# A conditioned transformer block on one Trainium2 core: another order of the products inside a block of tokens, and another place for the residual rows of odd blocks

## The chip, the cores and the metric

The kernel runs on one core of one Trainium2 chip. Its engines are TensorE (PE in the profile, its weight loads PEld), VectorE (DVE), ScalarE (ACT), GpSimd (POOL) and SyncE (SP), which issues nearly all the transfers here. The metric is the device time of one execution in microseconds (us). The time before is the median of three runs.

## What is computed

x has 8 sequences of T = 1024 tokens and D = 512 features, in float32. A condition vector for each sequence gives six modulation vectors. The reference, cut to its core:

```python
mod = silu(condition) @ Wada + bada
sh_a, sc_a, gt_a, sh_m, sc_m, gt_m = split(mod, 6, axis=1)
xm = layernorm(x, g1, be1) * (1 + sc_a) + sh_a
q, k, v = split(xm @ Wqkv)              # 16 heads of 32 features
a = softmax(causal(q @ k.T / sqrt(32))) @ v
x = x + gt_a * (a @ Wproj + bproj)
xm = layernorm(x, g2, be2) * (1 + sc_m) + sh_m
x = x + gt_m * (gelu(xm @ W1 + b1) @ W2 + b2)   # 512 -> 2048 -> 512, exact gelu
```

## The kernel before

**Tiles.** The work is cut into NB = 16 blocks of TB = 512 tokens, two for a sequence. An even block n is the first half of its sequence, an odd block the second half, whose queries also attend to the keys of the even block before it. Each linear product (q, k, v, the attention's projection, the four up products u0 to u3 of the MLP) is done with seven half-size products instead of eight, by sums of operands (Strassen-Winograd, `strassen`, L896; its last two products run as a side thread, `tail`). The sums of the weights are made once and kept in DRAM; "preps" and "sums" steps make them in the first windows. The four down parts d0 to d3 (`down`, L1196) take differences of the hidden tiles hT (L1211) and add their partial results to the residual rows. `matmul` (L205) issues four matmuls side by side on columns of TensorE; each is two records in the trace ("128*32" is this column form, "32*128" the row form of the attention's products over 32 features).

**Weights** come in pieces of 256 KB, in the order of the plan, on SP's queue into a ring of nine buffers "w" (`fetch`, L336 to L348). A buffer is loaded again when its piece is released.

**Attention** of a block goes through four groups of four heads (`attend`, L1824). For a group: scores in PSUM (L1602); DVE masks the diagonal units (L1616) and reduces each query's maximum (L1619; L1633 joins the two halves' maxima for odd blocks); the maxima are split into three bf16 parts (`split_maxima`, L1638 to L1641), on POOL or on DVE, whichever the planner's clocks say; TensorE turns them into rows (L1657) and ACT copies those (L1663). Then the transposed weights: the negative maxima are added by a product (L1683), the scores by another (L1695), ACT takes the exponential (L1708), POOL clears above the diagonal (L1713). TensorE multiplies by v (L1736), POOL or DVE add the weights up (L1821, L1818). Their sums come out of a product with ones (L1757) into one of three PSUM banks "l", which the linear products share; ACT takes the logarithm of it (L1767), copies the result (L1770), takes the exponential of the negative logarithm (L1775), and the product with that replaces the block's qT. For the last groups DVE does a part of that (L1782).

**Order of the work.** The kernel writes its instructions out in an order fixed while it is built. A hand-written `plan[w]` (L234) lists the linear steps of windows -1 to 16: in window w stands the attention of block w, and beside it go linear steps of the blocks around it. A planner keeps an estimated clock for each engine (`now`, `note`, `due`) and, before each attention step, lets linear work go ahead until the attention's next operand should be there or until the linear work done keeps pace with the planned share (`step_aside`, `pace`, `linear_wait`). `either` (L154) puts an addition of two tiles on DVE (L162) or POOL (L165) by the same clocks. GELU goes to ACT in excursions of four (L1153), each between two loads of a function table (L1153, L145).

Steps of a window: "load_xr" fetches the four residual tiles of a block (L1353); "proj" projects and adds the residual, which also gives the second norm's statistics (L628, L637 to L640, L653); "mt" transposes the normed rows (L769) and applies the modulation (L778, L784), with the sums for the fast products (L792, L794); "at" does that for the first norm of a later block; "load_xa" and "norm_a" fetch and norm its rows. In the plan of before, an odd window w takes the steps left over, v of w, load_xr and proj of w-1, k of w+1, mt, q of w+1, u0 to u3, at, d0, d1; an even one begins with the left d2, d3, and leaves its u3, at and d's to the next.

**Buffers.** Key tiles kT have three buffers of one pool in turn; residual rows have one buffer "xr", which only the rows of block 14 leave for a key buffer. A step waits by flags such as "free for k", which `attend` sets when the attention of a block begins.

Of the kernel before, what the change touches and what calls it, by code (L numbers as in the profile page):

```python
# [22 lines left out]
def kernel(  # L23
# [36 lines left out]
    P = 128  # L60
# [177 lines left out]
        0: [("load_xa", 2), ("preps",), ("k", 1), ("norm_a", 2), ("gates", "a"), ("q", 1)]  # L238
        + [("mod", 4), ("at", 2), ("v", 1), ("mod", 3), ("gates", "m")],
    }  # L240
    late = []
    for w in range(1, NB):
        n = w - 1
        m = mlp_steps(n)
        even = blocks[n][1] == 0
        rows_a = [("rows", blocks[n][0], "a")] if even else []
        rows_m = [("rows", blocks[n][0], "m")] if even else []
        own = m[:1] + ([("load_xa", w + 2)] if w + 2 < NB else []) + m[1:3]
        own += [("norm_a", w + 2)] if w + 2 < NB else []
        if w == NB - 1:  # L250
            steps = late[:1] + [("load_xr", n)] + rows_a + [("proj", n), ("mt", n)] + late[1:]
            steps += [("v", w)] + rows_m + own + m[3:6]
            late = m[6:]
        else:

            steps = late + [("v", w), ("load_xr", n)] + rows_a + [("proj", n), ("k", w + 1)]
            if w == 1:
                steps = [("load_xr", n)] + rows_a + [("k", w + 1), ("proj", n)]
            steps += [("mt", n), ("q", w + 1)] + rows_m + own
            at = [("at", w + 2)] if w + 2 < NB else []  # L260
            if blocks[w][1] == 0:

                late = m[3:4] + at + m[4:]
            else:
                steps += m[3:4] + at + m[4:6]
                late = m[6:]
        plan[w] = steps
    n = NB - 1
    plan[NB] = [("load_xr", n), late[0], ("beside", ("proj", n)), late[1], ("mt", n)] + mlp_steps(n)

    plain_proj = (NB - 2, NB - 1)
    kept_sums = {}
# [538 lines left out]
        return bank  # L811

    qTs, kTs, vs = {}, {}, {}
    projected, valued = set(), set()
    xm_of, hTs, hidden = {}, {}, set()

    SUMS = (("S1", "A21", "A22", ALU.add), ("S2", "S1", "A11", ALU.subtract),
# [78 lines left out]
    def strassen(step, x, dest, target, row, done, put=None, after={}):  # L896
# [91 lines left out]
        tail_key[0] = key  # L988
        start(tail())

    def project_T(step, store, pool, tag, done):

        n = step[1]
        dst = pool.tile([P, NC, TB], F32, tag=tag, name=f"{tag}_{n}")
        store[n] = dst
        yield from strassen(
            step,
            f"a{n}",
            lambda f, t: dst[:, half(f, 2), half(t, HB)],
            (tag, n),  # L1000
            False,
            done,
        )
# [326 lines left out]
    def perform(step):  # L1330
# [12 lines left out]
        elif kind == "load_xr":  # L1343
            n = step[1]
            b, h = blocks[n]
            if n == NB - 2:
                xr = kvp.tile([P, NTT, D], F32, tag="kT", name=f"xr_{n}")
            else:
                xr = xrp.tile([P, NTT, D], F32, tag="xr", name=f"xr_{n}")
            residual[n] = xr  # L1350
            for t in range(NTT):
                r0 = h * TB + t * P
                nc.sync.dma_start(xr[:, t, :], x[b, r0 : r0 + P, :])  # L1353
                landed = max(now["PE"], stored.get(n, 0.0)) + LANDING + 700 * t
                written["xr", n, t] = landed
        elif kind == "norm_a":
            key = f"a{step[1]}"
# [5 lines left out]
        elif kind == "beside":  # L1363
            start(perform(step[1]))
        elif kind == "sums":
            sum_weights(step[1:])
        elif kind == "mt":
            n = step[1]
            guards = [("v done", n + 1)]
            start(modulated(f"m{n}", *columns_of["m"], blocks[n][0], guards))  # L1370
        elif kind == "k":
            yield [("free for k", step[1])], []
            yield from project_T(step, kTs, kvp, "kT", lambda: None)
        elif kind == "q":
# [449 lines left out]
    def attend():  # L1824
        previous = None
        for n in range(NB):
# [19 lines left out]
            stream["rate"] = planned_time(n) / mine * (0.7 if n == 0 else 1.0)  # L1846
            written["free for k", n + 2 if n % 2 else n + 1] = 0.0
            written["free for k", n + 1] = 0.0
            for g, k, n_slots, upto in slots:
                if (n, g) == groups[-1]:  # L1850
                    margin[0] = -2000
# [47 lines left out]
            finish(n, g)  # L1899

    def next_scores():
        until(lambda: units[unit_at[0]][0] in projected)
        scores(*units[unit_at[0]])
        unit_at[0] += 1

# [12 lines left out]
    needs = sum(exp_need(parts) for n in range(NB) for g in range(NC) for parts in weight_units(n, g))  # L1918
    needs += sum(score_need(*unit) for unit in units)
    for n in range(NB):  # L1920
        written["attended", n] = NEVER
# [81 lines left out]
```

## Time and profile before

| | before |
|---|---|
| runs, median (range) | 3483.92 us (3483.72 to 3483.95) |
| profiled execution | 3487.44 us |
| its span | 3485.7 us |
| outside the span | 1.7 us |
| instructions on DVE, ACT, POOL | 2136, 1420, 2209 |
| bytes moved | 466.84 MB |

The profile is of one execution. Its page gives each engine's busy time and share of the span, 40 slices with the TensorE clock that was granted, the chain of work that ended last, and the costliest groups of instructions. The trace behind it answers further views: waits (engine, line waited for, total us, times, longest), windows (busy time of each engine in a stretch of time, then the granted clock, the share of DMA time and GB/s), and a timeline (start, duration, engine, line, operation, output and input; in brackets the idle time of the engine just before, and what ended it). Rows of a timeline on TensorE overlap a little, since matmuls are pipelined: the time that a group costs is the next row's start less its own.

### The profile page before, as it was taken

The page shows a single profiled execution, that of the slowest core. Times are in us where ns is not written, and L with a number is a line of the kernel's source. Part 1 is how long each engine was busy: PE and PEld are TensorE (multiplying, and loading weights), DVE is VectorE, ACT ScalarE, POOL GpSimd, SP SyncE. Part 2 cuts the span into 40 slices and gives each one's busy share as a digit, 9 for nine tenths or more (in the row PEclk, how much of TensorE's full clock was granted, in tenths as well). Part 3 has the DMA queues.
Part 4 walks back from the last instruction along what each step waited for, and adds up shares of the span by engine and source line. Part 5 has one row for each costly group of instructions (what it writes and reads, how often), then busy time and mean ns, then how long its engine had stood idle before and what let it go on. Part 6 is the DMA issues. An engine that isn't in the chain of part 4 may idle for free.

```text
span 3485.7 us, 122756 instructions
## 1 busy us (share of the span) xinstructions
PE 3448.3 (99%) x55618; PEld 1776.1 (51%) x55618; DVE 1905.0 (55%) x2136; ACT 1286.7 (37%) x1420; POOL 2074.5 (60%) x2209
## 2 busy tenths in 40 slices
PE   8999999999999999999999999999999999999999
PEld 5544455445554554545545455454554545545445
DVE  6765664554645556465564655645546455554463
ACT  2335243352433524235152352514524244241531
POOL 3676755675466664576645766557664576644640
PEclk9999999999999999999999999999999999999999
DMA  6843334335353353633536335363443534435334
GB/s 213 271 144 86 117 110 150 120 105 172 107 167 102 105 174 104 186 95 100 173 98 186 98 111 159 101 186 98 129 140 101 183 101 135 130 100 153 90 121 136
DMA packets 350523, 466.84 MB, mean 134 GB/s; under 512 B 27460, under 2 KB 212092, under 8 KB 350004
## 3 DMA queue, kind: packets, MB, share of 16 engines
q1 hardware_dynamic: 349808, 458.73, 43.8%
q8 instruction: 438, 7.18, 0.9%
q14 instruction: 81, 0.66, 0.1%
q10 hardware_dynamic: 196, 0.28, 0.0%
HBM read 416.90 MB, written 41.99 MB: 132 GB/s over the span
## 4 chain that ended last, share of the span: by engine, by line
PE 94%; DVE 3%; POOL 1%; ACT 1%; issue 0%; DMA 0%; SPq 0%; DVEq 0%; ACTq 0%; POOLq 0%
PE bank L205 65%; PE sc L1602 9%; PE po L1736 8%; PE st L1695 7%; PE st L1683 3%; DVE mx L1619 2%; PE bank L1757 2%; PE bank L769 1%; PE bank L1657 1%; POOL pT L1821 0%; DVE sc L1616 0%; POOL mcols L1640 0%; DVE pT L1818 0%; POOL mcols L1641 0%; DMA ada<-in_L_cond_Wada_dram 0%
## 5 line engine op out<-in xcount | busy, mean ns | idle before, releaser
L1821 POOL TENSOR_TENSOR pT<-pT,pT 128x256 f32<-128x256 f32 (+3 forms) x1254 | 1174.5, 972 | 210.3 <-ACT pT L1708 119.2
L1708 ACT ACTIVATE pT<-st 128x2048 f32<-128x2048 f32 x288 | 541.1, 1879 | 1001.1 <-PE st L1695 908.8
L205 PE MATMUL bank<-w,hT 128*32 128x256 f32 x14336 | 795.5, 379 | 0.0
L1619 DVE TENSOR_REDUCE mx<-sc 128x4 f32<-128x2048 f32 (+3 forms) x384 | 665.6, 1754 | 140.3 <-PE sc L1602 133.7
L205 PEld LDWEIGHTS bank<-w,hT 128*32 128x32 f32 x14336 | 448.8, 110 | 335.6 <-issue 29.2
L205 PE MATMUL bank<-xm_m,w 128*32 128x256 f32 x8192 | 498.8, 380 | 0.0
L205 PE MATMUL bank<-t_m,w 128*32 128x256 f32 x6144 | 384.2, 380 | 0.1
L205 PEld LDWEIGHTS bank<-xm_m,w 128*32 128x32 f32 x8192 | 253.6, 110 | 238.8 <-issue 76.0
L1713 POOL TENSOR_SCALAR_AFFINE_SELECT pT<-pT 128x512 f32<-128x512 f32 x256 | 164.8, 661 | 308.8 <-ACT pT L1708 306.9
L1602 PE MATMUL sc<-kT,qT 32*128 32x512 f32 (+3 forms) x3072 | 329.1, 520 | 2.9 <-DVE mx L1619 1.9
L1616 DVE TENSOR_TENSOR sc<-sc,mask 128x1024 f32<-128x1024 f32 (+1 forms) x160 | 162.9, 1018 | 276.2 <-PE sc L1602 217.6
L1736 PE MATMUL po<-pT,v 128*32 128x512 f32 (+3 forms) x3072 | 306.0, 493 | 0.0
L1695 PE MATMUL st<-qT,kT 32*128 32x512 f32 (+3 forms) x3072 | 299.8, 486 | 0.0
L205 PEld LDWEIGHTS bank<-t_m,w 128*32 128x32 f32 x6144 | 193.0, 110 | 180.8 <-issue 54.2
L205 PE MATMUL bank<-xm_a,w 128*32 128x256 f32 x3968 | 248.8, 381 | 1.3 <-ACT xm_a L784 1.1
L197 DVE TENSOR_TENSOR hT<-bank,u_u 128x512 f32<-128x512 f32 x192 | 129.1, 686 | 151.2 <-PE bank L205 149.0
L165 POOL TENSOR_TENSOR qT<-top,rec 128x512 f32<-128x512 f32 x60 | 77.1, 1285 | 219.8 <-ACT rec L1775 219.8
L1602 PEld LDWEIGHTS sc<-kT,qT 32*128 32x128 f32 x3072 | 129.4, 183 | 150.9 <-ACT pT L1708 61.8
L205 PE MATMUL bank<-w,qT 128*32 128x256 f32 (+1 forms) x2944 | 191.4, 399 | 1.3 <-DVE qT L1782 1.3
L1153 ACT ACTIVATE hT<-hT,cols 128x512 f32<-128x512 f32 x256 | 164.2, 711 | 55.0 <-DVE hT L197 54.4
L205 PE MATMUL bank<-t_a,w 128*32 128x256 f32 x2944 | 183.3, 380 | 0.0
L165 POOL TENSOR_TENSOR hT<-hT,hT 128x1024 f32<-128x1024 f32 x28 | 79.7, 2868 | 167.6 <-DVE hT L1211 167.6
(232 smaller groups left out, 3507.5 us busy)
## 6 DMA issues: line engine op xcount, KB each, us to landing
w<-in_L_cond_W_dram SPq DMA_DIRECT2D x384, 256.0 KB, 2.9
w<-kept_up_S SPq DMA_DIRECT2D x256, 256.0 KB, 2.6
w<-kept_down_S SPq DMA_DIRECT2D x256, 256.0 KB, 2.8
w<-kept_qkv_S SPq DMA_DIRECT2D x180, 256.0 KB, 2.7
w<-in_L_cond_Wqkv_dram SPq DMA_DIRECT2D x147, 256.0 KB, 3.0
hat<-in_x_dram SPq DMA_DIRECT2D x64, 256.0 KB, 4.7
xr<-in_x_dram SPq DMA_DIRECT2D x64, 256.0 KB, 4.6
out_dram<-xr SPq DMA_DIRECT2D x64, 256.0 KB, 2.6
```

Source lines behind the costliest of these rows:

```text
L165: nc.gpsimd.tensor_tensor(out, a, b, op)
L197: nc.vector.tensor_tensor(out, src, other, op)
L205: nc.tensor.matmul(ps[r, :], lhsT[:, r], rhs, start=start, stop=stop, skip_group_check=True)
L1153: nc.scalar.activation(hT[:, i, :], hT[:, i, :], AF.Gelu, bias=cols[:, O_B1 + f : O_B1 + f + 1])
L1602: nc.tensor.matmul(sc[:, j, c0 : c0 + w], qTs[n][r, gg, ts(qt, P)], keys_of(n, kh)[r, gg, :w], start=True, stop=True, skip_group_check=True,)
L1616: nc.vector.tensor_tensor(place, place, shape_of.to_broadcast(place.shape), ALU.add)
L1619: nc.vector.tensor_reduce(maxima[n, gg][:, kh, qt, :], sc[:, :, c0 : c0 + w], axis=AX.X, op=ALU.max)
L1695: nc.tensor.matmul(st[:, j, c0 : c0 + w], kT[r, gg, ts(k % NTT, P)], qT[r, gg, TB - w :], start=False, stop=True, skip_group_check=True,)
L1708: nc.scalar.activation(pT[:, :, :used], st[:, :, :used], AF.Exp, scale=scale)
L1713: nc.gpsimd.affine_select(diagonal, diagonal, pattern=[[0, HPG], [1, P]], compare_op=ALU.is_ge, fill=0.0, base=0, channel_multiplier=-1,)
L1736: nc.tensor.matmul(po[r, TB - w :], v[:, k % NTT, g * P + j * hd : g * P + (j + 1) * hd], pT[:, j, c0 : c0 + w], start=(k == 0), stop=last ...
L1821: nc.gpsimd.tensor_tensor(into, into, pT[:, j, c0 : c0 + w], ALU.add)
```

## The change

The plan of windows 1 to 15 is put in another order, so that the four down parts of a block stand together. In the new plan an odd window w (from 3) has: the left u2, u3 and "at"; load_xr and v; proj and mt of block w-1; d0 to d3 of block w-2; q, then k, of block w+1; u0 to u3 of w-1 with load_xa and norm_a among them; at. An even window has the same without the left steps ahead, and stops after u1 of its block, which leaves u2, u3 and at to the next window. In window 15, which has no q and k to make, d0 and d1 of block 14 come at the end; windows 1 and 2 lead over from the order of the first ones, and window 16 is as it was.

Key tiles get buffers by name: one for odd blocks and two for even blocks in turn. The residual rows of an odd block go into the even key buffer that is free at that time, for which load_xr waits for a new flag "free for xr"; the rows of even blocks use "xr". `next_scores` also asks that the keys are done, since k now comes after q. The planner's estimate of when residual rows land uses the stores of the block before.

```diff
+        at = [("at", w + 2)] if w + 2 < NB else []
+        ups = m[:1] + ([("load_xa", w + 2)] if w + 2 < NB else []) + m[1:3]
+        ups += ([("norm_a", w + 2)] if w + 2 < NB else []) + m[3:4] + at
+        head = rows_a + [("load_xr", n)]
+        if w == 1:
+            steps = head + [("k", w + 1), ("proj", n), ("mt", n), ("q", w + 1)]
+        elif w == 2:
+            steps = downs[2:] + [("v", w)] + head + [("proj", n), ("mt", n), ("q", w + 1), ("k", w + 1)]
+        elif w < NB - 1:
+            steps = late + head + [("v", w), ("proj", n), ("mt", n)] + downs + [("q", w + 1), ("k", w + 1)]
+        else:
+            steps = late + head + [("v", w), ("proj", n), ("mt", n)] + downs
+        cut = m[2] if blocks[w][1] == 0 else None
+        i = ups.index(cut) if cut in ups else len(ups)
+        plan[w] = steps + rows_m + ups[:i]
+        late, downs = ups[i:], m[4:]
+        if w == 1:
+            plan[w] += downs[:2]
         if w == NB - 1:
-            steps = late[:1] + [("load_xr", n)] + rows_a + [("proj", n), ("mt", n)] + late[1:]
-            steps += [("v", w)] + rows_m + own + m[3:6]
-            late = m[6:]
-        else:
-
-            steps = late + [("v", w), ("load_xr", n)] + rows_a + [("proj", n), ("k", w + 1)]
-            if w == 1:
-                steps = [("load_xr", n)] + rows_a + [("k", w + 1), ("proj", n)]
-            steps += [("mt", n), ("q", w + 1)] + rows_m + own
-            at = [("at", w + 2)] if w + 2 < NB else []
-            if blocks[w][1] == 0:
-
-                late = m[3:4] + at + m[4:]
-            else:
-                steps += m[3:4] + at + m[4:6]
-                late = m[6:]
-        plan[w] = steps
+            plan[w] += late + downs[:2]
+            downs = downs[2:]
     n = NB - 1
-    plan[NB] = [("load_xr", n), late[0], ("beside", ("proj", n)), late[1], ("mt", n)] + mlp_steps(n)
+    plan[NB] = [("load_xr", n), downs[0], ("beside", ("proj", n)), downs[1], ("mt", n)] + mlp_steps(n)
...
+    def key_tag(n):
+        return "odd_kT" if n % 2 else f"even_kT_{n // 2 % 2}"
...
-        dst = pool.tile([P, NC, TB], F32, tag=tag, name=f"{tag}_{n}")
+        if tag == "kT":
+            dst = pool.tile([P, NC, TB], F32, tag=key_tag(n), name=f"{tag}_{n}", bufs=1)
+        else:
+            dst = pool.tile([P, NC, TB], F32, tag=tag, name=f"{tag}_{n}")
...
-            if n == NB - 2:
-                xr = kvp.tile([P, NTT, D], F32, tag="kT", name=f"xr_{n}")
+            if n % 2:
+                yield [("free for xr", n)], []
+                spare = key_tag(min(n + 3, NB))
+                xr = kvp.tile([P, NTT, D], F32, tag=spare, name=f"xr_{n}", bufs=1)
             else:
                 xr = xrp.tile([P, NTT, D], F32, tag="xr", name=f"xr_{n}")
...
-                landed = max(now["PE"], stored.get(n, 0.0)) + LANDING + 700 * t
+                landed = max(now["PE"], stored.get(n - 1, 0.0)) + LANDING + 700 * t
...
-            yield from project_T(step, kTs, kvp, "kT", lambda: None)
+            yield from project_T(step, kTs, kvp, "kT", lambda: keyed.add(step[1]))
...
+            written["free for xr", n - 1] = 0.0
...
-        until(lambda: units[unit_at[0]][0] in projected)
+        until(lambda: units[unit_at[0]][0] in projected & keyed)
```

More of the change, by code (lines that the diff above doesn't have):

```diff
@@ L240 @@
     }
-    late = []
+    late, downs = [], []
     for w in range(1, NB):
@@ L247 @@
         rows_m = [("rows", blocks[n][0], "m")] if even else []
-        own = m[:1] + ([("load_xa", w + 2)] if w + 2 < NB else []) + m[1:3]
-        own += [("norm_a", w + 2)] if w + 2 < NB else []
-        if w == NB - 1:
-            steps = late[:1] + [("load_xr", n)] + rows_a + [("proj", n), ("mt", n)] + late[1:]
-            steps += [("v", w)] + rows_m + own + m[3:6]
-            late = m[6:]
-        else:
-            steps = late + [("v", w), ("load_xr", n)] + rows_a + [("proj", n), ("k", w + 1)]
-            if w == 1:
-                steps = [("load_xr", n)] + rows_a + [("k", w + 1), ("proj", n)]
-            steps += [("mt", n), ("q", w + 1)] + rows_m + own
-            at = [("at", w + 2)] if w + 2 < NB else []
-            if blocks[w][1] == 0:
-                late = m[3:4] + at + m[4:]
-            else:
-                steps += m[3:4] + at + m[4:6]
-                late = m[6:]
-        plan[w] = steps
+        at = [("at", w + 2)] if w + 2 < NB else []
[16 more added lines that the diff above has]
+            plan[w] += downs[:2]
+        if w == NB - 1:
+            plan[w] += late + downs[:2]
+            downs = downs[2:]
     n = NB - 1
-    plan[NB] = [("load_xr", n), late[0], ("beside", ("proj", n)), late[1], ("mt", n)] + mlp_steps(n)
+    plan[NB] = [("load_xr", n), downs[0], ("beside", ("proj", n)), downs[1], ("mt", n)] + mlp_steps(n)
     plain_proj = (NB - 2, NB - 1)
@@ L813 @@
     qTs, kTs, vs = {}, {}, {}
-    projected, valued = set(), set()
+    projected, keyed, valued = set(), set(), set()
     xm_of, hTs, hidden = {}, {}, set()
@@ L1920 @@
     for n in range(NB):
+        written["free for xr", n] = 0.0 if n == NB - 1 else NEVER
         written["attended", n] = NEVER
```

## The prediction

> **What bounds the kernel now.** I read the page first, for the engine that fills the span.
>
> ```profile
> span 3485.7 us, 122756 instructions
> PE 3448.3 (99%) x55618; PEld 1776.1 (51%) x55618; DVE 1905.0 (55%) x2136; ACT 1286.7 (37%) x1420; POOL 2074.5 (60%) x2209
> PEclk9999999999999999999999999999999999999999
> PE 94%; DVE 3%; POOL 1%; ACT 1%; issue 0%; DMA 0%; SPq 0%; DVEq 0%; ACTq 0%; POOLq 0%
> ```
>
> TensorE is busy for 99% of the span at the full granted clock (all nines), and 94% of the chain that ended last is its own work. A new order of the same products can only win back its idle time. The windows view says how much there is, stage by stage (columns: window, length, then PE's busy time):
>
> ```profile
> 920.00:1348.00 428.00, 426.64 (x6952) 219.37 (x6944) 229.95 (x258) 162.15 (x178) 263.47 (x279) 1.00 0.45 132
> 1348.00:1776.00 428.00, 426.64 (x6948) 219.37 (x6944) 230.04 (x259) 161.45 (x177) 263.00 (x279) 1.00 0.45 132
> 3150.00:3400.00 250.00, 246.69 (x3884) 126.19 (x3880) 126.79 (x138) 89.93 (x104) 130.59 (x123) 1.00 0.39 118
> ```
>
> A pair of blocks (even, then odd) takes 428 us, repeats exactly, and leaves 428.00 - 426.64 = 1.36 us of idle time; the tail window leaves 3.31 us. The waits view of one pair names it (total us, times, longest):
>
> ```profile
> PE bank L1657 <- POOL mcols L1641: 0.7, 1, 0.7
> PE bank L769 <- ACT xm_m L784: 0.3, 1, 0.3
> PE sc L1602 <- DVE mx L1619: 0.2, 1, 0.2
> ```
>
> The timeline shows why the longest of them, for the split maxima, is late, and prices a few things used below:
>
> ```profile
> 980.76 1.15 PE L1602 MATMUL sc<-kT,qT 32*128 32x384 f32 x16
> 981.84 1.50 PE L205 MATMUL bank<-t_m,w 128*32 128x256 f32 x24
> 982.05 1.23 DVE L1616 TENSOR_TENSOR sc<-sc,mask 128x1024 f32<-128x1024 f32 x1 [0.89 <-PE sc L1602]
> 983.16 2.77 PE L205 MATMUL bank<-w,hT 128*32 128x256 f32 x48
> 983.32 2.35 DVE L1619 TENSOR_REDUCE mx<-sc 128x4 f32<-128x1536 f32 x2
> 985.87 0.40 PE L1683 MATMUL st<-mrow,minus_ones 32*128 32x384 bf16 x8
> 986.40 2.35 DVE L1211 TENSOR_TENSOR hT<-hT 128x1024 f32<-128x1024 f32 x2
> 986.57 1.16 POOL L1640 CAST mcols<-rest 128x16 bf16<-128x16 f32 x1
> 988.93 0.41 PE L1657 MATMUL bank<-ident_b,mcols 128*32 128x128 bf16 x16 [0.74 <-POOL mcols L1641]
> 989.16 2.12 PE L205 MATMUL bank<-w,hT 128*32 128x256 f32 x36
> ```
>
> Scores end, DVE masks and reduces, POOL splits the maxima while DVE's two L1211 run, and TensorE has only 6.2 us of other work meanwhile. Two prices: a linear record costs (983.16 - 981.84) / 24 = 0.055 us; and since neighbouring rows overlap (988.93 + 0.41 ends 0.18 us after 989.16), a wait loses that overlap too. With it the pair's stalls cost about 0.92 (maxima), 0.38 (transposes L769), 0.25 and 0.18 (scores waiting for the reduction): 1.73 us.
>
> **What the change moves.** I count in the order of each engine's instructions as the changed kernel is built. TensorE's order is the same up to about 555 us of this trace, then differs in every block to the end, with the same matmuls in the same forms. Forms alternate a little more: 17 more column-to-row switches, each about 0.07 us (the 48 records from 983.16 to 985.87 take 2.71 where 48 x 0.055 is 2.64), at most 1.2 us, and 15 fewer runs of transposes, whose switches work the other way: between -1 and 1.2, and I take +0.1, since the two counts nearly cancel. The weights are the same; so are the DMAs, 1721.
>
> *What goes.* In an odd block 9.2 us of TensorE work, not 6.2, now lie between scores and the maxima's use, so the 0.92 goes; the second norm's transposes come with other work around them (0.38), and the scores of both blocks follow later (0.25 + 0.18). Six places each: 6 x 1.73 = 10.4 us. The tail's own stalls:
>
> ```profile
> 3203.66 1.89 PE L769 MATMUL bank<-ident,xh_m 128*128 128x128 f32 x13 [0.31 <-ACT xh_m L653]
> 3334.71 0.40 PE L1683 MATMUL st<-mrow,minus_ones 32*128 32x512 bf16 x4 [1.52 <-ACT pT L1708]
> 3358.86 1.07 PE L205 MATMUL bank<-w,qT 128*32 128x512 f32 x8 [1.07 <-DVE qT L1782]
> 3360.14 2.35 PE L205 MATMUL bank<-w,qT 128*32 128x512 f32 x20 [0.21 <-DVE qT L1782]
> ```
>
> With overlap and switches they cost about 0.8, 1.6 and 1.9, with 0.5 of smaller ones 4.8 us; they go because block 14's down products now stand behind the second norm and some 32 us of them between the last attention and its projection. Gain at most 10.4 + 4.8 = 15.2 us, 0.4% of the span. That is the bound below, since nothing but idle time can be won.
>
> *What is late instead.* Five pairs (blocks 5/6 to 13/14) repeat one order.
>
> A, odd block, third group: behind its last score unit stand 48 linear records (2.7 us) where the trace above has 24 + 48. The chain there, 981.84 to 985.87, takes 4.03 us: mask, two reductions, hops. Late 1.1 to 1.3; I take **1.2**.
>
> B, even block, second group: a bank is freed by the logarithm L1767, behind an exponential and a GELU excursion in ACT's queue:
>
> ```profile
> 1202.99 1.88 ACT L1708 ACTIVATE pT<-st 128x2048 f32<-128x2048 f32 x1 [1.62 <-PE st L1695]
> 1204.88 1.28 ACT L1153 ACT_TABLE_LOAD   x1
> 1206.18 2.56 ACT L1153 ACTIVATE hT<-hT,cols 128x512 f32<-128x512 f32 x4
> 1208.76 1.28 ACT L145 ACT_TABLE_LOAD   x1
> 1215.72 0.57 ACT L1767 ACTIVATE rec<-bank 128x512 f32<-128x512 f32 x1
> 3339.37 1.07 PE L1736 MATMUL po<-pT,v 128*32 128x512 f32 x8
> ```
>
> 1.88 + 1.28 + 2.56 + 1.28 + 0.57 = 7.6, with hops 7.7; TensorE has 72 linear records (3.9), a score unit (981.84 - 980.76 = 1.1), one weighted sum (1.07 less the 0.18 of overlap, 0.9) and the sums of L1757, of the same size (0.9): 6.8. Late **0.9**; the hops are not shown for this place, so 0.5 to 1.2.
>
> C, odd block, first to second group: one full reduction behind two combines and a small offset, against 64 records (3.6 us):
>
> ```profile
> L1619 DVE TENSOR_REDUCE mx<-sc 128x4 f32<-128x2048 f32 x192 | 439.6, 2290 | 137.0 <-PE sc L1602 133.7
> L197 DVE TENSOR_TENSOR hT<-bank,u_u 128x512 f32<-128x512 f32 x192 | 129.1, 686 | 151.2 <-PE bank L205 149.0
> ```
>
> 2.29 + 2 x 0.69 + hops = 3.7 to 4.1: late 0.1 to 0.5, taken **0.3**. D, even block: L1211 takes turns with POOL as at 986.40: 0 to 0.35, taken **0.2**.
>
> E, the splits. The planner puts the split of the maxima on DVE for 12 groups instead of one (new are the first groups of six even blocks, 4 to 14, and the second ones of five, 6 to 14), and 69 more instructions stand on DVE, 95 fewer on POOL. The one such split in the trace, with POOL adding weights beside it:
>
> ```profile
> 369.55 5.39 PE L205 MATMUL bank<-w,hT 128*32 128x256 f32 x96
> 372.78 4.99 POOL L1821 TENSOR_TENSOR pT<-pT,pT 128x512 f32<-128x512 f32 x4
> 373.30 0.83 DVE L1638 CAST mcols<-mx 128x16 bf16<-128x16 f32 x1
> 374.16 1.18 DVE L1639 TENSOR_TENSOR rest<-mx,mcols 128x16 f32<-128x16 f32 x1
> 376.62 1.23 DVE L1641 TENSOR_TENSOR mcols<-rest,mcols 128x16 bf16<-128x16 f32 x1
> ```
>
> and the third of the four where POOL does it, over the whole span:
>
> ```profile
> L1640 POOL CAST mcols<-rest 128x16 bf16<-128x16 f32 x63 | 22.5, 357 | 4.0
> ```
>
> Four operations on 16 columns take 376.62 + 1.23 - 373.30 = 4.55 us on DVE, each about as long as one of POOL's 1.25 us adds; from the scores' end at 369.55 to the split's end 8.3 us. On POOL the longer ones take 0.36 each (L1640 above), or 1.16 while L1211 runs (986.57). The distances in TensorE work are 6.5 us in the first groups (8.7 in block 4's) and 11.4 down to 4.8 in the second. So a first group is late by nothing if POOL is out of adds (373.30 - 369.55 = 3.75, and four short operations), by 8.3 - 6.5 = 1.8 if not. POOL there has four adds left and ends them about when the reduction ends; I take 0.2 to 0.3, **0.25** a pair. In the second groups POOL waits for ACT then, and DVE runs alone: 0.
>
> The Trainium skill, "SBUF — State Buffer", section "SBUF: two separate sides", speaks against this part: DVE and GpSimd share a pair of ports as an exclusive lock, held for a whole instruction, and the other fully blocks. The rows at 372.78 to 376.62 agree with it, 0.83 to 1.23 us for 16 columns. By the rule in every one of these groups, the sum would be rival 1's.
>
> First changed pair about 0.3, the tail's new last hop (a DVE copy behind four others, then the projection) 1.6: 1.9 us.
>
> *Transfers.* The odd blocks' residual rows leave ahead of v and wait for the freed key buffer, and a waiting transfer holds what is queued behind it on SP.
>
> ```profile
> w<-kept_down_S SPq DMA_DIRECT2D x256, 256.0 KB, 2.8
> xr<-in_x_dram SPq DMA_DIRECT2D x64, 256.0 KB, 4.6
> ```
>
> Counting TensorE work between the release of a ring buffer and the first matmul that reads its next content, less these landings, the tightest weight keeps about 7 us, as before. I cost this at nothing; if that cover is gone, see rival 3.
>
> **Sum**: 5 x (1.2 + 0.9 + 0.3 + 0.2 + 0.25) = 14.2, + 1.9 + 0.1 = 16.2 against 15.2: **+1.0 us**. The profiled execution is 3487.44 (span 3485.7 and 1.7 around it), 3.5 above the median of 3483.92. It becomes 3488.4, the median **3485.0**. With low ends (A 1.1, B 0.5, C 0.1, D and E 0) the pairs lose 8.5 and the time is 3479; with high ends (1.3, 1.2, 0.5, 0.35, E 1.8) 25.8 and 3497.
>
> **Rivals.**
> 1. *Slower: POOL's adds stretch the DVE splits.* The mechanism is row 373.30's, in the first groups of even blocks. It decides once POOL has three or more 1.25 us adds queued when the reduction ends. Then each group is late by 1.8: 5 x (1.8 - 0.25) = 7.8 more, 3493. If the second groups meet it too, the two tightest are late by 8.3 - 4.8 = 3.5: 3500; and 3509 if the bank copies that stand behind the split make all five so late by 3.3. For: 11 new splits on DVE; against: POOL has 95 instructions less.
> 2. *Faster: late spots covered.* The stalls go as said, and A and B vanish as well because the counted chains start earlier than I place them. Left are C, D, E and the 2.0: 5 x 0.75 + 2.0 = 5.75, so -9.5, 3474.5. For: such orders fit in most places of before; against: A and B are chains of rows with no slack to hide.
> 3. *The weight queue.* A residual transfer waiting for its key buffer holds SP for more than 7 us. If the cover of 7 us is gone in six odd blocks and each is late by one landing of 4.6: +28, 3513. Against: the key buffer is free once the next block's attention starts, and SP is many pieces ahead.
>
> That the change does nothing is excluded by the order as built.
>
> **How the numbers follow.** Forecast (stalls change places) 0.74, rival 1 0.14, rival 2 0.09, rival 3 0.03. A measurement tells 0.2%, 7 us, from no change: below 3477 is faster, above 3491 slower. So faster 0.09, same 0.74, slower 0.17. The range reaches from 3477, between the forecast's low end and rival 2, to 3496, which holds rival 1's first form and the sum's high ends.
>
> **What would show it.** Right: no wait of L1657 for POOL at odd second groups; L1683 waiting for DVE about 1.2 us once a pair, a bank waiting for L1767 about 0.9; no 1.52 and 1.07 in the tail; PE busy within 2 us of 3448.3, so that the span moves only by idle time. Wrong: rows of L1638 to L1641 on DVE at 0.8 to 1.2 us followed by a wait of L1657 (rival 1), pairs of 426.6 (rival 2), waits of L205 for a DMA into w (rival 3), or a clock below 1.00.

## The result, and the profile after

The changed kernel takes 3510.5 us (median of 4 runs, 3507.82 to 3511.5) where the kernel before takes 3483.82 (3483.01 to 3483.95): 26.7 us or 0.76% slower, ratio 1.0076, 95% interval 1.0058 to 1.0093. The forecast was 3485, the range ended at 3496. The profiled execution took 3511.21 us. Its page:

```profile
span 3509.4 us, 122646 instructions
PE 3458.1 (99%) x55618; PEld 1786.3 (51%) x55618; DVE 2022.8 (58%) x2205; ACT 1287.5 (37%) x1436; POOL 2051.2 (58%) x2114
PE 91%; DVE 4%; ACT 3%; POOL 1%; DMA 1%; issue 1%; SPq 0%; ACTq 0%; DVEq 0%; POOLq 0%
```

TensorE does the same 55618 records, but is busy for 9.8 us longer (3458.1 against 3448.3), and idle for 13.9 us longer (51.3 against 37.4). So part of the loss is not waiting: the same work ran slower. DVE is busy for 118 us more though only 69 instructions were added. Two pairs of blocks in the middle, each from one row of maxima (L1666 of an odd block's third group) to the same row of the next pair (length, PE's busy time, then the others):

```profile
1070.22:1503.69 433.47, 428.62 (x6946) 222.06 (x6946) 252.24 (x271) 161.87 (x181) 258.21 (x262) 1.00 0.43 130
1503.69:1936.32 432.63, 428.40 (x6944) 222.16 (x6945) 251.78 (x272) 161.60 (x180) 258.19 (x262) 1.00 0.43 130
```

A pair takes 431.3 to 433.5 us (the two after these 432.70 and 431.31) instead of 428. The waits of one pair (1340 to 1773 us), total, times, longest:

```profile
PE bank L1666 <- POOL mcols L1650: 2.1, 1, 2.1
PE bank L205 <- ACT rec L1776: 1.5, 2, 0.9
PE st L1692 <- DVE mx L1628: 1.2, 2, 1.1
```

(Lines behind the plan are 1 to 9 higher than in the kernel before: L1218 is L1211, L1666 is L1657, L1650 is L1641, L1628 is L1619, L1776 is L1767, L1642 is L1633.) The three waits of before are gone, and others stand there. The last two lines are B (0.91 each pair, and one more at times) and A (1.09, with one of 0.15 at C's place) of the prediction. The first, 2.07 us, isn't in its sum. Nor is this one, of the stretch from 400 to 920 us:

```profile
PE sc L1611 <- ACT pT L1717: 3.6, 1, 3.6
```

The timeline of an odd block shows where the 2.07 us come from:

```profile
1490.29 1.15 PE L1611 MATMUL sc<-kT,qT 32*128 32x256 f32 x16
1490.60 3.50 DVE L1218 TENSOR_TENSOR hT<-hT,hT 128x1024 f32<-128x1024 f32 x2
1490.87 6.58 POOL L1830 TENSOR_TENSOR pT<-pT,pT 128x512 f32<-128x512 f32 x3
1494.02 2.30 DVE L162 TENSOR_TENSOR hT<-hT,hT 128x1024 f32<-128x1024 f32 x1
1496.24 1.22 DVE L1625 TENSOR_TENSOR sc<-sc,mask 128x1024 f32<-128x1024 f32 x1
1498.65 2.36 POOL L165 TENSOR_TENSOR hT<-hT,hT 128x1024 f32<-128x1024 f32 x1
1499.76 1.28 DVE L1642 TENSOR_TENSOR mx<-mx 128x16 f32<-128x16 f32 x1
1501.11 0.65 POOL L1647 CAST mcols<-mx 128x16 bf16<-128x16 f32 x1
1502.60 0.69 POOL L1649 CAST mcols<-rest 128x16 bf16<-128x16 f32 x1
1503.69 0.41 PE L1666 MATMUL bank<-ident_b,mcols 128*32 128x128 bf16 x16 [2.07 <-POOL mcols L1650]
1505.50 2.44 PE L205 MATMUL bank<-w,hT 128*32 128x256 f32 x24
```

These are the scores of the third group. When they end (1491.36), DVE has three differences of hidden tiles of part d1 ahead of their mask, which take 3.50 + 2.30 us beside POOL's adds; the mask starts 4.9 us late. Then DVE's L1642, on 16 columns, takes 1.28 us and ends 0.03 us behind POOL's operation of 2.36 us, and three of POOL's four splits take 0.65 to 0.69 beside DVE's operations. The same join of the two halves' maxima in the kernel before, with POOL idle:

```profile
985.70 0.17 DVE L1633 TENSOR_TENSOR mx<-mx 128x16 f32<-128x16 f32 x1
```

Last, the row behind the wait: 24 linear records in 2.44 us, where 24 take 1.48 elsewhere in this trace. The windows there give the granted clock (third number from the end):

```profile
1500.00:1504.00 4.00, 1.93 (x52) 1.13 (x48) 3.83 (x6) 1.88 (x1) 3.68 (x6) 1.00 0.35 123
1504.00:1508.00 4.00, 4.00 (x44) 1.33 (x36) 3.96 (x2) 0.59 (x1) 4.00 (x3) 0.57 0.00 0
```

Behind the wait TensorE runs at half its clock for some 3.4 us ((1 - 0.57) x 4 / 0.5), and loses 1.7 us by it. In this execution that happened behind four of the five 2.07 us waits and for 5.6 us behind the wait of 3.6 us. Together these stretches lose 6.8 + 2.8 = 9.6 us, which is nearly all of the 9.8 us that TensorE was busy longer. The page's row of clock digits, all nines, is too coarse to show it.

### The profile page after: what moved, and what is told of

It is laid out like the page before. It is cut to its first block, busy times and chain, and to the rows that moved or that the text cites. A ratio compares the mean times of both kernels' runs of the same rounds, so it can differ in the third digit from the quotient of the medians.

```text
span 3509.4 us, 122646 instructions
## 1 busy us (share of the span) xinstructions
PE 3458.1 (99%) x55618; PEld 1786.3 (51%) x55618; DVE 2022.8 (58%) x2205; ACT 1287.5 (37%) x1436; POOL 2051.2 (58%) x2114
## 4 chain that ended last, share of the span: by engine, by line
PE 91%; DVE 4%; ACT 3%; POOL 1%; DMA 1%; issue 1%; SPq 0%; ACTq 0%; DVEq 0%; POOLq 0%
PE bank L205 63%; PE sc L1611 8%; PE po L1745 7%; PE st L1704 7%; PE st L1692 3%; DVE mx L1628 2%; PE bank L1766 2%; ACT pT L1717 1%; PE bank L770 1%; ACT hT L1160 1%; DVE sc L1625 1%; PE bank L1666 1%; ACT L145 0%; ACT L1160 0%; DMA xm_a<-turned_a 0%
## 5 line engine op out<-in xcount | busy, mean ns | idle before, releaser
L1830 POOL TENSOR_TENSOR pT<-pT,pT 128x256 f32<-128x256 f32 (+3 forms) x1254 | 1247.1, 1030 | 200.8 <-ACT pT L1717 130.8
L1717 ACT ACTIVATE pT<-st 128x2048 f32<-128x2048 f32 x288 | 540.9, 1878 | 1036.9 <-PE st L1704 956.7
L205 PE MATMUL bank<-w,hT 128*32 128x256 f32 x14336 | 823.1, 381 | 0.6 <-ACT rec L1776 0.6
L1628 DVE TENSOR_REDUCE mx<-sc 128x4 f32<-128x2048 f32 (+3 forms) x384 | 665.7, 1754 | 190.1 <-PE sc L1611 183.9
L205 PEld LDWEIGHTS bank<-w,hT 128*32 128x32 f32 x14336 | 453.7, 110 | 367.2 <-issue 86.1
L205 PE MATMUL bank<-xm_m,w 128*32 128x256 f32 x8192 | 499.9, 380 | 0.0
L205 PE MATMUL bank<-t_m,w 128*32 128x256 f32 x6144 | 383.7, 380 | 4.7 <-ACT rec L1776 4.5
L205 PEld LDWEIGHTS bank<-xm_m,w 128*32 128x32 f32 x8192 | 255.4, 110 | 222.9 <-issue 60.2
L205 PEld LDWEIGHTS bank<-t_m,w 128*32 128x32 f32 x6144 | 190.2, 110 | 181.9 <-issue 53.2
L205 PE MATMUL bank<-xm_a,w 128*32 128x256 f32 x3968 | 240.8, 381 | 1.3 <-ACT xm_a L785 1.1
L205 PE MATMUL bank<-w,qT 128*32 128x256 f32 (+1 forms) x2944 | 194.8, 401 | 0.0
L205 PE MATMUL bank<-t_a,w 128*32 128x256 f32 x2944 | 180.0, 379 | 0.0
L205 PEld LDWEIGHTS bank<-xm_a,w 128*32 128x32 f32 x3968 | 126.7, 110 | 98.7 <-issue 16.6
L1160 ACT ACTIVATE hT<-hT,cols 128x512 f32<-128x512 f32 x256 | 163.8, 711 | 27.4 <-DVE hT L197 26.8
```

The source lines that it names most:

```text
L205: nc.tensor.matmul(ps[r, :], lhsT[:, r], rhs, start=start, stop=stop, skip_group_check=True)
L1160: nc.scalar.activation(hT[:, i, :], hT[:, i, :], AF.Gelu, bias=cols[:, O_B1 + f : O_B1 + f + 1])
L1628: nc.vector.tensor_reduce(maxima[n, gg][:, kh, qt, :], sc[:, :, c0 : c0 + w], axis=AX.X, op=ALU.max)
L1717: nc.scalar.activation(pT[:, :, :used], st[:, :, :used], AF.Exp, scale=scale)
L1830: nc.gpsimd.tensor_tensor(into, into, pT[:, j, c0 : c0 + w], ALU.add)
```

## The experiments

**Theory.** The loss comes from the order: in five odd blocks the third group's maxima are late, because differences of hidden tiles stand ahead of their mask and POOL and DVE hold each other up; a wait of that size lowers the clock; and one wait of 3.6 us stands in block 3. **Rivals:** the new buffers and their transfers; the 12 splits of maxima on DVE; a crowd caused by the second norm's sums. Times are medians; the kernel before is measured again beside each group of runs.

**The buffers alone**, with the plan of before:

```diff
+            dst = pool.tile([P, NC, TB], F32, tag=key_tag(n), name=f"{tag}_{n}", bufs=1)
...
+                yield [("free for xr", n)], []
+                xr = kvp.tile([P, NTT, D], F32, tag=spare, name=f"xr_{n}", bufs=1)
```

> The kernel before with only the buffer part of the change: keys in buffers by name, the residual rows of odd blocks in the free key buffer with the flag they wait for, and the new landing estimate; the plan is the old one, and the order of the instructions on PE, DVE, ACT and POOL is that of before. Theory (the loss comes from the order: a late split of maxima in five odd blocks, a lowered clock behind it, one late transfer's consumer in block 3): within 2 us of before, 3482 to 3486. Rival (the residual rows in the key buffers hold the queue and delay transfers): a good part of the 26.7 us shows here, 3490 or more, with waits of L205 or L1602 for a DMA.

3484.11 us against 3485.44, ratio 0.9996 (0.9987 to 1.0006). In the old order the buffers and the wait for them cost nothing. In the new order TensorE's waits past the start-up name no transfer, and one hangs on one by way of ACT (block 4's turned rows, below). So the order is what costs.

**The mask first.** The planner's choices and TensorE's order stay; only DVE's and POOL's instructions change places. While `hold` is set, additions and differences go into a list, and `let_go` issues them:

```diff
+            hold[0] = n % 2 == 1
             combine(nc.vector, "B22", "B22", "B12")
             combine(nc.gpsimd, "B11", "B22", "B11")
+            hold[0] = False
             bank, ps = yield from product("B21")
+            let_go()
...
             split_maxima(n, g, h)
+        let_go()
```

> The changed kernel, with one thing moved: the first differences of hidden tiles in part d1 of odd blocks (two on DVE, the next two) stand behind the mask and the reductions of the scores recorded beside them, not ahead of them. PE, ACT and all else keep their order. Theory: these differences hold DVE for 5.8 us when the scores of an odd block's third group are ready, so that its maxima are split late; without them the five waits of 2.07 us fall under 0.5 us, and with them the stretches of half clock behind four of them: 5 x 2.14 + 6.8 = 17.5 us less, 3493 (3490 to 3497). Rival (the splits themselves are stretched by POOL's and DVE's other work, or transfers are late): the waits stay above 1.5 us and the time falls by less than 4 us.

3508.18 us against 3485.44, ratio 1.0066 (1.0051 to 1.0081). The five waits and the slow stretches behind them are gone, as the theory has it, but the time hardly moved. Waits of one pair, and the row of the new one (this kernel's lines are higher again: L216 is L205, L1791 is L1776, L1781 is the sums of L1766):

```profile
PE bank L216 <- ACT rec L1791: 2.8, 2, 1.9
PE st L1707 <- DVE mx L1643: 1.2, 2, 1.1
PE bank L1781 <- POOL pT L1845: 1.0, 1, 1.0
```

```profile
1515.30 5.93 POOL L1845 TENSOR_TENSOR pT<-pT,pT 128x384 f32<-128x384 f32 x7
1520.05 2.29 PE L1781 MATMUL bank<-pT,ones 128*32 128x512 f32 x8 [1.02 <-POOL pT L1845]
```

Some 16 us after the cured place TensorE waits for POOL's adds: 1.02 us, and the sums themselves take 2.29 instead of 1.04, since each add is awaited. Laid record by record against the changed kernel's trace, the cure gives 2.1 us at each of the five waits and 1.6 to 1.7 for each of the four slow stretches; 2.1 to 2.4 come back at the sums each time, 2.1 once at a new wait in the first changed pair, and in one pair 3.0 at a wait for L1791 with a slow stretch of its own. So the late maxima look like one face of a fuller cause: DVE and POOL have too much to do there. From the third group's last scores to the use of its maxima (busy times of PE, PEld, DVE, ACT, POOL), in the changed kernel, and then the same length from the same scores in the kernel before:

```profile
1490.29:1503.69 13.40, 11.33 (x182) 6.84 (x178) 13.23 (x12) 7.38 (x9) 13.00 (x11) 1.00 0.35 99
1098.54:1111.94 13.40, 13.10 (x196) 7.03 (x196) 9.87 (x10) 6.84 (x9) 11.32 (x15) 1.00 0.30 89
```

DVE and POOL together were busy for 26.2 of 26.8 engine-microseconds, against 21.2. Busy time holds the time for which one keeps the other up, so it shows the crowd, not the work.

**Work in the place of waiting**, to see whether the wait lowers the clock:

```diff
             bank = lin_bank()
+            if n % 2 and n > 3 and n < NB - 1 and g == 2:
+                for _ in range(6):
+                    for qt in range(NTT):
+                        for j in range(HPG):
+                            r = slice(j * hd, (j + 1) * hd)
+                            nc.tensor.matmul(
+                                banks[bank][r, ts(qt, P)], ident_b[:, r], ident_b,
+                                start=True, stop=True, skip_group_check=True,
+                            )
             for qt in range(NTT):
```

> The changed kernel with 96 small extra matmuls (bf16, identity by identity, into the bank that the maxima's rows overwrite right after) ahead of the maxima's rows in the third group of odd blocks 5 to 13, about 1.4 us of TensorE work in the place of waiting. Theory (a wait of about 2 us lowers the granted clock to 0.50 for some 3.5 us behind it): the rows of the maxima start at the same time, the wait before them falls to about 0.6 us, the granted clock stays at 1.00 there, and the four slow stretches of about 1.7 us go: 6.8 us less, about 3503.7 (3502 to 3506). Rival (the slow stretches come from something else, such as DVE or POOL work or the weights): the stretches stay, 3510 or more.

3506.81 us against 3485.44, ratio 1.0062 (1.0047 to 1.0077), just above the expected range. No slow stretch stands behind any of the five places; the intervals of the times overlap, so the gain itself rests on the trace. Its rows, and the clock:

```profile
1498.36 1.52 PE L1668 MATMUL bank<-ident_b 128*32 128x128 bf16 x96
1500.49 0.41 PE L1675 MATMUL bank<-ident_b,mcols 128*32 128x128 bf16 x16 [0.61 <-POOL mcols L1650]
1501.58 1.47 PE L205 MATMUL bank<-w,hT 128*32 128x256 f32 x24
```

```profile
1500.00:1504.00 4.00, 3.51 (x56) 1.38 (x56) 3.93 (x3) 1.03 (x2) 3.92 (x4) 1.00 0.01 4
```

The 24 records take 1.47 us again.

**Waits of growing length in the kernel before:**

```diff
+        if g == 1:
+            for _ in range({3: 2, 5: 3, 7: 4, 9: 5, 11: 6, 13: 8}.get(n, 0)):
+                engine.tensor_tensor(rest, m, high, ALU.subtract)
```

> The kernel before, with the split of the maxima of the second group of odd blocks lengthened by repeating its subtraction 2, 3, 4, 5, 6 and 8 times more in blocks 3, 5, 7, 9, 11 and 13, on POOL. Theory: the waits of L1657, 0.74 us each before, grow by 0.25 to 0.4 us a repetition, from about 1.4 to about 3.3 us, and the granted clock falls to 0.50 behind those that pass about 2 us (three of the six), each of which costs 1.7 us beyond its wait: in all some 9 + 5 = 14 us more than before. Rival (the clock has nothing to do with the waits): no slow stretch, 9 us more.

One run, 3495.24 us. The waits came out at 1.39, 1.70, 2.00, 2.30, 2.61 and 3.21 us, and only the last lowered the clock:

```profile
2276.00:2280.00 4.00, 3.18 (x72) 1.93 (x76) 0.02 (x1) 3.58 (x6) 1.76 (x5) 1.00 0.11 35
2709.00:2713.00 4.00, 4.00 (x48) 1.93 (x44) 0.00 (x0) 0.85 (x2) 0.00 (x0) 0.58 0.20 70
```

So the expected bound of 2 us was wrong: 2.61 us here left the clock at 1.00, where 2.07 halved it at four of five places in the first profile of the changed kernel. The last section shows what decides.

**All splits on POOL:**

```diff
-        engine = nc.gpsimd if on_pool else nc.vector
+        engine = nc.gpsimd
```

> The changed kernel with all splits of maxima on POOL; the 12 groups that the planner gives to DVE are the only difference, and the order of everything else stays. Rival 1 of the prediction (those splits on DVE are what is slow): 5 to 15 us less than the changed kernel, 3500 to 3506 on a chip where before takes 3484. Theory (they run in 0.2 us each on DVE while POOL is idle, and cost nothing; the loss sits in the third group of odd blocks, where POOL and DVE have too much to do between them): within 3 us of the changed kernel, 3508 to 3513, the five waits of about 2 us for L1650 on POOL unchanged.

3513.26 us against 3484.43, ratio 1.0078 (1.0061 to 1.0095): no gain. Rival 1 falls. In the changed kernel itself a split on DVE in an even block's second group took 0.2 us an operation, while POOL waited for ACT (one operation took 1.33 once). In the first groups, where POOL adds weights, two of the four operations took 0.40 and 1.18 us, but TensorE waited at none of them. The rows of a second group also show B, a bank freed late by the logarithm:

```profile
1631.19 0.60 ACT L1776 ACTIVATE rec<-bank 128x512 f32<-128x512 f32 x1
1631.57 0.20 DVE L1647 CAST mcols<-mx 128x16 bf16<-128x16 f32 x1
1631.84 1.93 PE L205 MATMUL bank<-t_m,w 128*32 128x256 f32 x32 [0.91 <-ACT rec L1776]
```

**The second norm's transposes behind the down parts:**

```diff
-            steps = late + head + [("v", w), ("proj", n), ("mt", n)] + downs + [("q", w + 1), ("k", w + 1)]
+            steps = late + head + [("v", w), ("proj", n)] + downs + [("mt", n), ("q", w + 1), ("k", w + 1)]
```

> The changed kernel with one step of the plan moved: the transposes of the second norm stand behind the four down parts, not ahead of them; q and k follow. Theory (DVE and POOL are crowded because the second norm's sums, the differences of the hidden tiles and the attention's adds fall into the same 40 us of the odd block): the crowd is thinned, the 2 us waits for the maxima in five odd blocks go, and 8 to 17 us with them, 3494 to 3503. Rival (any order with the four down parts together is as slow, since the same DVE and POOL work meets the same third group): within 4 us of the changed kernel, 3507 to 3514.

3499.18 us against 3484.43, ratio 1.004 (1.0025 to 1.0055). The time is as expected, but by luck, since the reason is not: the five waits stay, at 2.11 us, so the second norm's sums don't cause them. What went are the five waits of A (1.09 each) and, in this execution, all slow stretches but one.

**The down parts between q and k** instead of ahead of both:

```diff
-            steps = late + head + [("v", w), ("proj", n), ("mt", n)] + downs + [("q", w + 1), ("k", w + 1)]
+            steps = late + head + [("v", w), ("proj", n), ("mt", n), ("q", w + 1)] + downs + [("k", w + 1)]
```

> The changed kernel with the four down parts between q and k, not ahead of q. Theory: the second norm's sums are done beside q, the differences come later, and the waits of the odd third groups go; others may come, 3490 to 3505. Rival (as for the run before): 3507 to 3514.

3614.79 us against 3484.43, ratio 1.0373. Both expectations fail. Scores of the next block must wait for its keys, and stand in a row then with no linear work between: 26 waits of L1692 for the reductions, 64.6 us in all. The granted clock, 0.989 over the whole span, takes some 40 us more.

**The changed kernel again, and two single cures beside it:**

> The changed kernel once more, unchanged, so that the three others stand beside it on one chip. 3508 to 3513, with the waits of its first profile.

3508.36 us against 3485.00, ratio 1.0068 (1.0053 to 1.0083). The five waits are the same, 2.06 to 2.08 us; this time only two of them lowered the clock, with no instruction changed.

```diff
                 pT, slot = weights_T(n, g, parts)
-                run_excursions(1)
+                if not (h == 0 and previous is not None and previous[5]):
+                    run_excursions(1)
```

> The changed kernel without the GELU excursion between the exponential and the logarithm where an even block's group ends (it goes at the next place instead). Theory (B of the prediction): the five waits of 0.91 us of L205 for L1776 go, 5 x 1.12 = 5.6 us less than the changed kernel, 3505; the other waits stay. Rival: the excursion delays the next GELUs and a wait of the same size shows elsewhere, within 2 us of the changed kernel.

3515.69 us, ratio to before 1.0091 (1.0076 to 1.0106): 7.3 us above the kernel beside it, whose interval it overlaps, and neither what was expected nor the rival. B is gone, as its waits in one pair show, but each pair has a late split of 1.6 us in its place, and A is 1.4 in this pair (the first line is the late maxima again; the split's last row and L1717 end close together, and here the wait is put down to the latter):

```profile
PE bank L1666 <- ACT pT L1717: 2.1, 1, 2.1
PE bank L1666 <- POOL mcols L1650: 1.6, 1, 1.6
PE st L1692 <- DVE mx L1628: 1.4, 1, 1.4
```

```diff
-            written["spread", key] = queue_free[0] + 5000
+            written["spread", key] = queue_free[0] + (8000 if key == "a4" else 5000)
```

> The changed kernel with the planner told that the turned rows of block 4 land 3 us later than it assumes, so that ACT is given their modulation later and the exponential ahead of it isn't held. Theory: the wait of 3.59 us near 583 us goes and with it the half clock behind it (2.7 us): 4 to 6.3 us less than the changed kernel, 3504 to 3507. Rival (the rows land late for all that reads them, so another wait takes its place): within 2 us of the changed kernel.

3506.35 us, ratio 1.0061 (1.0046 to 1.0076). The wait of 3.6 us (2.8 in the kernel beside it, whose clock stayed up there) is gone; the gain of 2.0 us is inside the intervals.

**Four cures at once:** moved transposes, mask first, no excursion ahead of the logarithm, later rows of block 4, all as above.

> The changed kernel with four edits at once: the second norm's transposes behind the down parts, the differences of odd blocks behind the mask, no excursion ahead of the logarithm, and the later landing of block 4's rows. Theory (the waits are local and add up): from 3499 of the moved transposes, less 5 x 2.1 for the splits, less 5.6 for the logarithm, less 3 for the rows: 3480, 3476 to 3486, that is level with before or a little faster. Rival (POOL and DVE together are the bound of the odd block's third group, so that a removed wait comes back at the sums for L1766, as behind the mask alone): 3490 or more.

3499.82 us against 3485.00, ratio 1.0042 (1.0026 to 1.0059): no better than the moved transposes alone. One pair of it:

```profile
PE bank L216 <- ACT rec L1791: 1.8, 1, 1.8
PE bank L1681 <- POOL mcols L1665: 1.6, 1, 1.6
PE st L1707 <- DVE mx L1643: 1.2, 2, 1.1
```

The rival's time holds, and half of its reason: a wait that is removed comes back as another, but hardly at the sums (L1781 waits for POOL once, 1.2 us). The 1.6 us are the late split that the removed excursion brought in the run before.

**A cure for the kernel before.** Its 0.74 us wait came from POOL's split beside DVE's differences. The split goes to DVE, ahead of them:

```diff
+        on_pool = on_pool and not (h and g == 1 and n > 1)
         engine = nc.gpsimd if on_pool else nc.vector
```

> The kernel before with the splits of the maxima of odd blocks' second groups on DVE, where two differences of hidden tiles on DVE stretch them on POOL (1.16 and 1.07 us in the profile of before). Theory (a short operation is stretched only while the other engine works beside it; POOL has just finished its adds there, so DVE's four operations take about 0.2 us each and stand ahead of the differences): the wait of 0.74 us for the maxima goes in six blocks, 5.5 us less than before, about 3478.5. Rival (DVE's splits take 0.8 to 1.2 us each, as in the one group of before that had them there): the wait grows to about 2.5 us, 10 us or more slower.

3478.61 us against 3484.43, ratio 0.9984 (0.9974 to 0.9993): faster than both kernels, and as forecast. The place that waited before:

```profile
980.71 0.20 DVE L1639 CAST mcols<-mx 128x16 bf16<-128x16 f32 x1
981.47 0.23 DVE L1642 TENSOR_TENSOR mcols<-rest,mcols 128x16 bf16<-128x16 f32 x1
982.17 2.35 DVE L1211 TENSOR_TENSOR hT<-hT 128x1024 f32<-128x1024 f32 x2
982.73 0.41 PE L1658 MATMUL bank<-ident_b,mcols 128*32 128x128 bf16 x16
```

No wait stands at the last row, and the split's ends take 0.2 us.

## Why the prediction was wrong

The two profiled spans differ by 23.7 us (the medians by 26.7). Laid against the usual price of each run of records, so that a wait counts with the overlap it loses:

| step | predicted | measured |
|---|---|---|
| stalls that go, pairs and tail | -15.2 | -15.2 |
| A, five times | 6.0 | 5.8 |
| B, five times | 4.5 | 5.6 |
| C and D, five times | 2.5 | 1.1 |
| E, splits on DVE | 1.25 | 0 |
| late maxima of third groups, five times 2.14 | none | 10.7 |
| half clock behind four of them | none | 6.8 |
| first changed pair | 0.3 | 8.6 |
| tail | 1.6 | 2.1, by another wait |
| start-up, the same code in both kernels | 0 | -3.2 |

The measured column adds up to 22.3; 1.4 us are spread over places under 0.2 us.

- *What bounds the kernel, and the gain of at most 15.2 us*: right. All the named stalls went.
- *A and B*: right, in place and size. Both were chains of rows, counted against the TensorE work beside them.
- *C, D and E*: smaller than taken, within their bounds. E priced the splits that moved to DVE; the late ones are those that stayed on POOL.
- *The step that failed*: "On POOL the longer ones take 0.36 each (L1640 above), or 1.16 while L1211 runs", and no more of it: splits left on POOL were in no term of the sum. In the order as built the third group of an odd block has 10.2 us of TensorE work between its scores and the use of its maxima, more than any place counted late, and has no term. But the chain took 12.3 us (1491.36 to 1503.69): it starts behind 5.8 us of differences in DVE's queue, and the two engines stretch each other. The distance was priced, the queue ahead of the mask was not. The prediction had this same pattern before it, at 986.40 to 988.93.
- *The tail's 1.6* was hit by luck. The hop that it priced, a DVE copy ahead of the projection, shows no wait. TensorE waits at another place, for a reduction that stands behind a stretched addition in DVE's queue, which is the failed step once more:

```profile
3171.40 3.21 DVE L162 TENSOR_TENSOR xr<-xr,y 128x512 f32<-128x512 f32 x1
3176.86 0.40 PE L1692 MATMUL st<-mrow,minus_ones 32*128 32x512 bf16 x4 [1.73 <-DVE mx L1628]
```

- *"First changed pair about 0.3"*: ACT starts on block 4's turned rows 7.3 us after their transfer is issued, having waited for them ahead of an exponential, and TensorE waits for 3.6 us, with 2.8 more lost to the clock. Moving that step later removed the wait.
- *The clock* was read off nine tenths in 40 slices and taken as constant, so it has no term; here it took 9.6 us, and the sign that PE stays busy within 2 us of 3448.3 failed with it. No wait of before past its start-up is over 1.6 us. At its start-up a slow stretch did stand behind a wait of 2.11 us, and could have warned:

```profile
25.00:28.20 3.20, 3.20 (x36) 2.05 (x32) 2.67 (x3) 0.00 (x0) 3.20 (x3) 0.50 0.96 275
```

- *Rival 1* gives 3493, 3500 or 3509 by splits on DVE at which no wait stands; that its time is near is chance. What it took from row 373.30, that each of the two engines stretches the other's short operations, did occur, at other places. *Rival 2* is refuted by A and B, which stood. *Rival 3* is refuted: the buffers alone cost nothing, and no wait of L205 for a transfer stands in the changed kernel.

The deeper cause is shown in part: curing the late maxima alone brings new waits of TensorE for POOL's adds, and curing four waits brings others. That this comes from the shared load of DVE and POOL in the odd block is argued from the busy times, not shown by an experiment that thins it; which regrouping of the steps would do so was not found. The profiles do show that the new order makes the two meet more often, since the same instructions take longer, here 32 of DVE's differences before and after:

```profile
L1211 DVE TENSOR_TENSOR hT<-hT 128x1024 f32<-128x1024 f32 x32 | 38.8, 1252 | 0.0
L1218 DVE TENSOR_TENSOR hT<-hT 128x1024 f32<-128x1024 f32 x32 | 53.6, 1716 | 0.0
```

POOL's 1254 adds of weights grew likewise, from 1178.5 to 1251.0 us. The Trainium skill, "SBUF — State Buffer", section "SBUF: two separate sides", states the lock by which one of the two waits for the other's whole instruction; the row of L1642, 1.28 us beside a POOL operation of 2.36, agrees.

## What to carry to other kernels

When an order changes, price for each consumer the whole queue ahead of its producer on that engine, not only the distance on the bounding engine: 10 us of distance was not enough for 3.6 us of masks and reductions with 5.8 us queued ahead. Short operations cost 0.2 us when the neighbour engine is idle and up to 1.3 beside its long ones, so put them where the other waits, as the split ahead of the differences did for 5.8 us. And add to a wait on TensorE of 2 us or more what the clock may take behind it, 1.7 us or more here.

## What the runs showed of the hardware

A wait of TensorE of about 2 us and more can halve its granted clock for 3.4 us or longer, and whether it does isn't set by its length alone. The same 2.07 us waits did so at four of five places in one execution of the changed kernel and at two of five in the next. In the kernel before with lengthened waits, 2.30 and 2.61 us left the clock alone.

What decides is where the wait falls. In the first profile of the changed kernel the falls past the start-up begin at 582.44, 1070.55, 1504.04, 1937.53 and 2801.11 us, that is 143, 127, 127 and 253 times 3.413 us apart; in every other trace with more than one fall they are whole multiples of 3.413 us apart too. These times are marks that cut the trace into windows. The first two rows are the window that holds the whole wait before 1503.69 and the one behind it. The next three are those around the equal wait before 2369.02, which a mark cuts into 0.67 and 1.40 us:

```profile
1500.63:1504.04 3.41, 1.34 (x43) 0.89 (x40) 3.24 (x6) 1.88 (x1) 3.09 (x6) 1.00 0.24 82
1504.04:1507.45 3.41, 3.41 (x32) 1.16 (x25) 3.38 (x2) 0.59 (x1) 3.41 (x2) 0.50 0.00 0
2364.21:2367.62 3.41, 2.74 (x52) 1.46 (x44) 3.31 (x4) 0.53 (x1) 3.24 (x3) 1.00 0.46 142
2367.62:2371.03 3.41, 2.01 (x44) 1.01 (x48) 3.31 (x5) 1.93 (x2) 3.27 (x5) 1.00 0.05 17
2371.03:2374.44 3.41, 3.41 (x56) 1.55 (x52) 3.41 (x2) 0.00 (x0) 3.41 (x2) 1.00 0.02 5
```

The 14 traces have 129 waits of TensorE over 1.3 us past the start-up. All 28 with at least 2.05 us inside one window were followed by a fall at its end, 7 of the 17 with 1.74 to 2.03, and none of the 84 with less. Those of 2.30 and 2.61 us were cut into 1.53 + 0.77 and 1.39 + 1.22. The marks lie elsewhere in each execution, so the same kernel loses a different time to the clock each time. That can widen the spread: 3.7 us between the changed kernel's runs, 0.9 between those of before beside it.

The Trainium skill, "TensorE: Matmul & The Clock Gate", section "Part 1: The HAM clock gate", puts the fall after an idle window of about 3.4 us and says that the hardware watches a free-running window. The marks agree with such a window; the idle time that it takes is less than the page says, since 2.05 us of 3.41 were enough here, and there the measurement decides.
